# A four-stage transformer block on one core: products of a fast matrix multiplication summed in PSUM by twos, the feed-forward norms transposed by TensorE, and a new instruction order

## The chip, the core and the metric

The kernel runs on one core of a Trainium2 chip. The metric is the device time of one execution in microseconds, lower is better; the figure for the kernel before is the median of three runs. Everything is fp32.

## The reference

Eight sequences of 512 rows and 256 columns go through four residual stages. Each stage normalises its input without weights, and its result is added to the input.

```python
x = x + attn_a(layernorm(x))   # linear attention: l2norm(xWq) * mean over rows of (l2norm(xWk) * xWv)
x = x + ffn(layernorm(x))      # sigmoid(xr Wr) * (relu(xk Wk)**2 Wv)
x = x + attn_b(layernorm(x))   # 16 heads of 64: softmax over axis=2 of q k^T / 8, then Wl, with biases
x = x + ffn(layernorm(x))      # the same weights as the first ffn
```

In the ffn, `xr = mu_r * x + (1 - mu_r) * x_prev` and `xk` likewise, where `x_prev` is the sequence shifted down by one row. In `attn_b` the softmax is taken along the queries, so its sums belong to keys and can scale the values.

## The kernel before, in words

A sequence is called b, its two halves of 256 rows are h. Names in the profile follow the stages: `a` is the norm of the linear attention, `f` the first ffn, `n` the norm of the head attention, `g` the second ffn. `tr_g` is thus a transposed norm of a second ffn, `k_g`, `r_g` and `o_g` its three products, `kv` and `q` the products of the linear attention, `y` the output projection of the heads.

**Head attention.** Heads go in pairs g, eight pairs for each sequence, 64 in all. For each pair and each of four blocks c of 128 keys, `scores` makes a 128x1024 tile `sc` in two banks of PSUM, VectorE takes the negated maxima `nm`, ScalarE writes the exponentials `e` with their sums, GpSimd scales the values (`vs`), and `context` accumulates `cx`. `attend` issues two pairs at once, each `context` behind the next `scores`. PSUM has three double tiles (`PAIRS`) and two single ones (`BANKS`); all other products take one of these five slots.

**Seven products.** The projections to q, k and v of the heads use a fast scheme with seven products of half-size blocks in place of eight. `project_pairs` makes q and k of two pairs, `values_fast` half of a sequence's values; both call `seven`, which is run 31 + 14 times. Sums of weights are made once, sums of rows (`xts`) once for each sequence. Each product has its own bank, and its result is read and added by VectorE, ScalarE (`L780` copies product 5) and GpSimd (`L783`, `L785` add product 5 to two partial results). The last two additions are `L788` and `L792`.

**Norms.** `normed` takes statistics on VectorE, the power on GpSimd and the scaled copy on ScalarE (or on VectorE, if `early`). The result is needed transposed. `normed_t` does that by TensorE, four 128x128 transposes into a bank. `normed_dma` does it by DMA: GpSimd splits the fp32 words into 16-bit halves (`L405`), the SP queue issues a transposing DMA, ScalarE joins the halves (`L414`). In the kernel before, a0, a1, f0, f1, n0, n1 and g7 are transposed by TensorE, all others by DMA. The ffn then makes the shifted part on ScalarE (`L465`) and mixes on VectorE (`L479`), from the bank or, behind the DMA, from SBUF.

**Order.** Every queue is in order, and the program is written in one sequence by a planner. `Order` keeps a clock for each engine ("T" TensorE, "A" ScalarE, "V" VectorE, "G" GpSimd, "S" the SP queue). Every strand of work is a generator whose `yield` names the engine, a cost in us, when it can start, and optionally a mark it waits for. The planner always runs the strand that can start first, with ties broken by due times and by `CHOICES`, one triple for each double pair: a share of TensorE work, a slack, and a seed of tie-breaking numbers. `attend` calls `fill`, which puts in work that fits within a slack; between two `attend` calls, `until` and `fill` issue the strands: projections for the next pairs, norms, ffns, linear attention.

```python
for first in range(0, G, 2):
    g = order.period = first + 1
    attend(first)
    ...
    order.add(project_pairs(g + 1), g, NP)
    ...
    order.until(g, share)
```

The next `attend` starts with the scores of pair g + 1, so they wait for the last addition of `seven` for these pairs.

Of the kernel before, what the change touches and what calls it, by code (L numbers as in the profile page):

```python
# [32 lines left out]
PASS = {"T": 0.27, "A": 0.2, "V": 0.17, "G": 0.17, "S": 2.0}  # L33
# [5 lines left out]
    (1, 1, 35120), (4, 0, 43370), (-1, 0, 57790), (-2, 2, 0), (-2, 0, 0), (-2, 2, 98886),  # L39
    (-6, 0, 75181), (-4, 2, 57617), (1, 2, 0), (6, -1, 74538), (-2, 2, 93122), (0, 0, 0),  # L40
    (-1, 2, 13389), (0, 2, 5382), (4, 0, 20720), (-4, 2, 0), (4, -1, 42679), (0, 0, 80313),
    (-1, -1, 6501), (-1, 1, 49947), (-6, -1, 38303), (0, 1, 13925), (0, 0, 0), (-2, 2, 98850),
    (4, 1, 69230), (0, -1, 54519), (4, 0, 64684), (-2, 0, 15869), (2, 2, 90925), (-4, 2, 75109),
    (6, 2, 43324), (-6, 2, 0), (0, 0, 0), (2, 2, 66685),
# [3 lines left out]
class Steps:  # L48

# [9 lines left out]
    def advance(self, end):  # L59
        try:  # L60
            step = self.gen.send(end)
        except StopIteration:
            self.live = False
            return
        self.live = True
        self.on, self.cost, self.ready = step[:3]
        self.gate = step[3] if len(step) > 3 else -1
        self.mark = step[4] if len(step) > 4 else None

# [5 lines left out]
class Order:  # L75
# [5 lines left out]
    def __init__(self):  # L81
        self.free = {"T": 0.0, "A": 0.0, "V": 0.0, "G": 0.0, "S": 0.0}
        self.chains, self.period, self.spent, self.count = [], -1, 0.0, 0
        self.marks = {None: 0.0}

        self.banks = [0.0] * (PAIRS + BANKS)
        self.current, self.at = None, 0.0
# [40 lines left out]
    def give(self):  # L128

        self.banks = [self.ended if c is self.current else c for c in self.banks]  # L130

    def ready(self, c):
        ready = max(c.ready, self.marks[c.mark])
        if c.on == "T":
            slots = self.slots(self.now)
            if slots:
                ready = max(ready, slots[0][0])
        return ready
# [4 lines left out]
    def run(self, c):  # L143
        if c.on == "T":
            self.spent += c.cost
        outer = self.current, self.at
        self.current, self.at = c, self.now
        end = self.ended = self.place(c.on, c.cost, self.ready(c))
        c.advance(end)
        self.current, self.at = outer  # L150
        if not c.live:
            self.chains.remove(c)

    def able(self, most=99.0):

        return [
            c for c in self.chains
            if c.mark in self.marks and c.gate <= self.period
            and (c.on != "T" or c.cost <= most and self.slots(self.now))
        ]  # L160
# [61 lines left out]
    def finish(self):  # L222
        self.period = 10**6
        while self.chains:
            self.run(self.first(self.able()))
# [3 lines left out]
def kernel(ctx: ExitStack, tc: tile.TileContext, a: dict, out: bass.AP):  # L229
# [119 lines left out]
    def normed(src, name, s, h, ready, early=False):  # L349
# [8 lines left out]
        if early:  # L358

            ready = yield "G", 1.05, ready  # L360
            nc.gpsimd.tensor_scalar(rstd, mv[:, :, 1], LN_EPS, 1.0, ALU.add, ALU.mult)
            nc.gpsimd.tensor_tensor(rstd, rstd, neg_half[:, :2], ALU.pow)
            ready = yield "V", 0.75, ready
            for u in range(2):
                nc.vector.tensor_scalar(
                    xn[:, u, :], src[:, 2 * h + u, :], mv[:, u, 0:1], rstd[:, u : u + 1],
                    ALU.subtract, ALU.mult,
                )
        else:

            shift = small.tile([P, 2], F32, tag="shift", name=f"shift_{name}_{h}")
            nc.vector.tensor_scalar(shift, mv[:, :, 0], -1.0, None, ALU.mult)
            ready = yield "G", 1.3, ready
            nc.gpsimd.tensor_scalar(rstd, mv[:, :, 1], LN_EPS, 1.0, ALU.add, ALU.mult)
            nc.gpsimd.tensor_tensor(rstd, rstd, neg_half[:, :2], ALU.pow)
            nc.gpsimd.tensor_tensor(shift, shift, rstd, ALU.mult)
            ready = yield "A", 1.0, ready
            for u in range(2):
                nc.scalar.activation(  # L379
                    xn[:, u, :], src[:, 2 * h + u, :], AF.Identity,  # L380
                    bias=shift[:, u : u + 1], scale=rstd[:, u : u + 1],
                )
# [15 lines left out]
    def normed_dma(src, name, s, h, ready, dst, mark=None):  # L398
# [4 lines left out]
        ready = yield "G", 1.8, ready  # L403
# [9 lines left out]
        ready = yield "A", 0.9, ready, -1, mark  # L413
        nc.scalar.copy(  # L414
# [26 lines left out]
    edge = {}  # L441

    def ffn(xb, name, s, h, ready, add_on, by_dma):


        if by_dma:
            ps = chunks(s["xr"], h)
            ready = yield from normed_dma(
                xb, name, s, h, ready,
                lambda: s["xr"].bitcast(U16)[:, h, :].rearrange("p (k s) -> p k s", k=KC),  # L450
            )
        else:
            ps, ready = yield from normed_t(xb, name, s, h, ready)

        parts = ((1, s["xn"]), (0, s["xp"]))
        if not edge:
            nc.gpsimd.tensor_scalar(fv, fv, 0.5, None, ALU.mult)
            order.place("G", 0.8, 0.0)
# [16 lines left out]
        xr, xk = chunks(s["xr"], h), chunks(s["xk"], h)  # L475
# [9 lines left out]
        if not by_dma:  # L485
            order.give()
        done = yield "T", BANK, mixed
# [32 lines left out]
    xta, vh, fronts, begun = {}, {}, set(), set()  # L520
# [29 lines left out]
    def linear(b, h):  # L550
# [4 lines left out]
        if b < 2:  # L555
            ps, ready = yield from normed_t(xb, f"a{b}", s, h, ready, early=True)
            ready = yield "A", 0.5, ready
            nc.scalar.copy(xt, ps)
            order.give()
        else:  # L560
            ready = yield from normed_dma(
                xb, f"a{b}", s, h, ready, lambda: s["xp"].bitcast(U16)[:, h, :, 2:]
            )
# [72 lines left out]
    def front(b, h, gf, ready):  # L636
# [10 lines left out]
        ready = yield from ffn(xb, f"f{b}", s, h, ready, adder(b), b >= 2)  # L647
# [104 lines left out]
    def seven(name, sums, mul, c, begin, join):  # L752
# [3 lines left out]

        (c11, c12), (c21, c22) = c

        def product(n):
            ready = yield "T", FAST, 0.0, -1, sums  # L760
            ps = bank(f"m{n}_{name}")
            mul(ps, n)
            return ps.rearrange("p (u s) -> p u s", u=2), ready

        ps, ready = yield from product(1)
        u1 = yield from begin(ps, c11, ready)
        order.give()
        ps, ready = yield from product(6)
        u2 = yield "V", 0.62, max(ready, u1)
        nc.vector.tensor_tensor(c12, ps, c11, ALU.add)  # L770
        order.give()
        ps, ready = yield from product(2)
        yield "V", 0.62, max(ready, u1)
        nc.vector.tensor_tensor(c11, ps, c11, ALU.add)
        order.give()
        ps, ready = yield from product(7)
        u3 = yield from join(ps, c21, c12, max(ready, u2))
        ps, p5 = yield from product(5)
        p5 = yield "A", 0.5, p5
        nc.scalar.copy(c22, ps)  # L780
        order.give()
        u6 = yield "G", 1.3, max(p5, u2)
        nc.gpsimd.tensor_tensor(c12, c12, c22, ALU.add)  # L783
        u7 = yield "G", 1.3, max(p5, u3)
        nc.gpsimd.tensor_tensor(c22, c22, c21, ALU.add)  # L785
        ps, ready = yield from product(4)
        yield "V", 0.62, max(ready, u7)
        nc.vector.tensor_tensor(c21, ps, c21, ALU.add)  # L788
        order.give()
        ps, ready = yield from product(3)  # L790
        order.marks[name] = max(u7, (yield "V", 0.62, max(ready, u6)))
        nc.vector.tensor_tensor(c12, ps, c12, ALU.add)  # L792
        order.give()
# [9 lines left out]
    def project_pairs(g):  # L803

        b, p = divmod(g, NP)
        lhs = [
# [6 lines left out]
        def mul(ps, n):  # L813
            for w in range(2):
                nc.tensor.matmul(  # L815
                    ps[:, w * HS : (w + 1) * HS], lhsT=lhs[w][n - 1], rhs=block_of_rows(b, n),
                    start=True, stop=True,
# [10 lines left out]
        def join(ps, dst, part, ready):  # L828
# [6 lines left out]
            order.give()  # L835
# [5 lines left out]
    def values_fast(b, half):  # L841


        rhs = blocks_of_weights(av, blocks["sums_v"], split_values, half)
        yield "G", 0.0, 0.0, -1, ("vs", NP * (b - 1) + 3 + 4 * half, 1)
        v = vh[b, half] = one.tile([P, NT, 512], F32, tag=f"v{half}", name=f"v_{b}_{half}")

        def mul(ps, n):
            for u in range(2):
                nc.tensor.matmul(  # L850
                    ps[:, u * HS : (u + 1) * HS], lhsT=block_of_rows(b, n)[:, u * P : (u + 1) * P],
                    rhs=rhs[n - 1], start=True, stop=True,
# [12 lines left out]
        def join(ps, dst, part, ready):  # L865
            ready = yield "V", 0.62, ready
            nc.vector.tensor_tensor(dst, ps, part, ALU.add)
            order.give()
            ready = yield "G", 1.3, ready
            nc.gpsimd.tensor_tensor(dst, dst, spread(dvb[:, half, :]), ALU.add)  # L870
# [49 lines left out]
    def tail(b, h, ready):  # L920
# [4 lines left out]
        yield from ffn(x[b], f"g{b}", buffers(not last), h, ready, add_on, not last)  # L925
# [111 lines left out]
    def attend(g):  # L1037

        for c in range(NT):
# [8 lines left out]
            order.fill(0.0, 2.8)  # L1048
        for c in range(NT):
# [8 lines left out]
            order.fill(0.0, 2.8)  # L1058
# [29 lines left out]
    total -= 6 * 3.3 + 7 * 1.1  # L1088
    total += 2 * FAST
    for first in range(0, G, 2):  # L1090
# [3 lines left out]
        order.place("T", CHANGE, 0.0)  # L1094
        for h in range(2):
# [69 lines left out]
```

## Time and profile before

| What | Value |
|---|---|
| median of 3 runs | 1161.8 us (1161.39 to 1164.65) |
| profiled execution | 1162.71 us, its span 1160.8 us |
| granted TensorE clock, mean | 0.994 |
| matmul passes | 7012 |
| transposing DMAs (`DMA_TRANSPOSE`), 3.1 us to landing | 50 |

The page of the profile gives the busy time of every engine; the groups of instructions have a line of the kernel, an engine, an operation, the tiles out<-in, a count, busy us and the mean ns of one. An fp32 matmul is shown as two passes, a transpose as one. The ends of matmuls are modelled, so their starts are the firmer figure. A wait is put down to what ended it.

### The profile page before, as it was taken

To read this page: it belongs to the slowest core of one execution; us is meant where nothing else is said; L and a number is where in the kernel's file an instruction comes from. 1 tells how busy PE (TensorE), PEld (TensorE's weight loads), DVE (VectorE), ACT (ScalarE), POOL (GpSimd) and SP (SyncE) were. 2 spreads that over 40 slices of the span, in tenths; PEclk is the share of its full clock that TensorE was granted. 3 is DMA by queue.
4 is the path that set the end of the run, shared out by engine and by line. 5 is a ranking of instruction groups with operands and counts; after the bars stand their busy time and mean duration, and the time that the engine had idled before them with its cause. 6 is when DMAs were issued, how large, how long until landed. Compare 5 with 4: busy or idle time off the path is not lost.

```text
span 1160.8 us, 19186 instructions
## 1 busy us (share of the span) xinstructions
PE 1129.8 (97%) x7012; PEld 703.9 (61%) x7012; DVE 806.4 (69%) x1384; ACT 730.6 (63%) x1802; POOL 485.7 (42%) x702
## 2 busy tenths in 40 slices
PE   6999899999999999999999999999999999999997
PEld 3646466655668566656666655766657655666556
DVE  5676776777866767776886667676776777656853
ACT  3666575677855767657585568456774776556643
POOL 5465434443337334345532444442546343433211
PEclk9999899999999999999999999999999999999999
DMA  8000000110102100012000120001110100000001
GB/s 294 1 1 19 1 19 2 28 20 9 19 1 64 37 1 19 1 46 38 10 10 10 46 38 1 10 19 37 24 32 15 24 11 10 19 10 11 10 1 37
DMA packets 63294, 29.17 MB, mean 25 GB/s; under 512 B 53568, under 2 KB 61760, under 8 KB 62688
## 3 DMA queue, kind: packets, MB, share of 16 engines
q1 hardware_dynamic: 62048, 26.22, 9.4%
q8 instruction: 56, 0.92, 0.3%
q10 hardware_dynamic: 864, 1.05, 0.3%
q0 software_dynamic: 288, 0.67, 0.2%
q14 instruction: 38, 0.31, 0.1%
HBM read 10.63 MB, written 4.19 MB: 13 GB/s over the span
## 4 chain that ended last, share of the span: by engine, by line
PE 46%; DVE 2%; issue 1%; ACT 1%; DVEq 0%
PE cx L1024 10%; PE sc L971 10%; PE m_qk L815 8%; PE y L426 5%; PE m_v L850 4%; PE r_g L426 2%; PE o_g L426 2%; PE k_g L491 1%; PE r_f L426 1%; PE kv L571 1%; PE o_f L426 1%; PE k_f L491 1%; PE q L426 1%; DVE xrFalse L479 1%; DVE xrTrue L479 0%
## 5 line engine op out<-in xcount | busy, mean ns | idle before, releaser
L987 ACT ACTIVATE e<-sc,nm 128x512 f32<-128x512 f32 x512 | 346.6, 690 | 126.7 <-DVE nm L976 125.5
L976 DVE TENSOR_REDUCE nm<-sc 128x2 f32<-128x1024 f32 x256 | 307.9, 1216 | 60.9 <-PE sc L971 60.5
L971 PE MATMUL sc<-qk 64*64 64x512 f32 x2048 | 270.5, 600 | 9.4 <-DVE qk L792 8.3
L1024 PE MATMUL cx<-e,vs 64*64 64x512 f32 x2048 | 268.2, 594 | 0.2 <-POOL vs L1004 0.2
L1004 POOL TENSOR_TENSOR vs<-v,rs 128x256 f32<-128x256 f32 x128 | 78.5, 614 | 383.2 <-DVE rs L1000 363.3
L1024 PEld LDWEIGHTS cx<-e,vs 64*64 64x64 f32 x2048 | 85.4, 134 | 139.9 <-issue 115.9
L971 PEld LDWEIGHTS sc<-qk 64*64 64x64 f32 x2048 | 73.8, 133 | 151.4 <-issue 82.7
L426 PE MATMUL y<-al,ctx 128*128 128x256 f32 x512 | 116.3, 380 | 0.0
L426 PEld LDWEIGHTS y<-al,ctx 128*128 128x128 f32 x512 | 96.8, 190 | 17.3 <-ACT e L987 3.2
L987 ACT ACTIVATION_READ_ACCUMULATOR e<-sc,nm 128x1 f32 x512 | 105.6, 206 | 0.0
L1032 DVE TENSOR_TENSOR ctx<-cx,ctx 128x512 f32<-128x512 f32 x64 | 44.2, 691 | 48.0 <-ACT ctx L1031 46.9
L571 PE MATMUL kv<-wkv,xpFalse 128*128 128x512 f32 x112 | 52.4, 607 | 1.1 <-ACT xpFalse L414 1.1
L783 POOL TENSOR_TENSOR qk<-qk,qk 128x512 f32<-128x512 f32 x31 | 40.8, 1315 | 27.8 <-ACT qk L780 26.2
L913 DVE TENSOR_TENSOR x<-y,x 128x512 f32<-128x512 f32 x32 | 22.1, 689 | 39.9 <-PE y L426 39.7
L405 POOL COPY xrFalse<-xnFalse 128x512 uint16<-128x512 uint16 x72 | 42.6, 626 | 8.1 <-ACT xnFalse L379 8.1
L1031 ACT COPY ctx<-cx 128x512 f32<-128x512 f32 x64 | 37.5, 585 | 12.3 <-PE cx L1024 12.3
L517 POOL TENSOR_TENSOR x<-x,xkFalse 128x512 f32<-128x512 f32 x24 | 31.0, 1293 | 29.5 <-DVE xkFalse L510 21.9
L785 POOL TENSOR_TENSOR qk<-qk 128x512 f32<-128x512 f32 x31 | 40.6, 1310 | 2.4
L815 PE MATMUL m_qk<-xts,aq 128*128 128x256 f32 x124 | 37.1, 381 | 3.9 <-DVE v L788 3.9
L815 PE MATMUL m_qk<-xta,aq 128*128 128x256 f32 x124 | 38.2, 390 | 0.0
L770 DVE TENSOR_TENSOR qk<-m_qk,qk 128x512 f32<-128x512 f32 x31 | 21.4, 691 | 23.9 <-PE m_qk L815 23.3
L815 PE MATMUL m_qk<-xta,sums_q 128*128 128x256 f32 x124 | 36.9, 379 | 0.0
(248 smaller groups left out, 2037.5 us busy)
## 6 DMA issues: line engine op xcount, KB each, us to landing
out<-x SPq DMA_DIRECT2D x16, 256.0 KB, 2.1
x<-in_x SPq DMA_DIRECT2D x6, 512.0 KB, 4.3
aq<-in_aq SPq DMA_DIRECT2D x1, 1024.0 KB, 7.9
ak<-in_ak SPq DMA_DIRECT2D x1, 1024.0 KB, 9.9
av<-in_av SPq DMA_DIRECT2D x1, 1024.0 KB, 11.9
al<-in_al SPq DMA_DIRECT2D x1, 1024.0 KB, 14.3
xkFalse<-xrFalse SPq DMA_TRANSPOSE x36, 3.1
x<-in_x SPq DMA_DIRECT2D x4, 128.0 KB, 4.3
```

The costliest lines, as they stand in the source:

```text
L405: nc.gpsimd.tensor_copy(apart.rearrange("p (l k u d) -> p l k u d", l=2, k=KC, u=2)[:, :, :, u, :], s["xn"].bitcast(U16)[:, h, u, 2:].rear ...
L426: nc.tensor.matmul(ps[:, u * D : (u + 1) * D], lhsT=lhs[i][:, u * P : (u + 1) * P], rhs=rhs[i], start=(i == 0), stop=(i == n - 1),)
L571: nc.tensor.matmul(ps, lhsT=xt[:, kc, u * P : (u + 1) * P], rhs=wkv[:, kc, :], start=(kc == 0), stop=(kc == KC - 1),)
L783: nc.gpsimd.tensor_tensor(c12, c12, c22, ALU.add)
L815: nc.tensor.matmul(ps[:, w * HS : (w + 1) * HS], lhsT=lhs[w][n - 1], rhs=block_of_rows(b, n), start=True, stop=True,)
L850: nc.tensor.matmul(ps[:, u * HS : (u + 1) * HS], lhsT=block_of_rows(b, n)[:, u * P : (u + 1) * P], rhs=rhs[n - 1], start=True, stop=True,)
L971: nc.tensor.matmul(ps[m * HD : (m + 1) * HD, j, :], lhsT=kt[hs, keys], rhs=qt[hs, :], start=True, stop=True,)
L976: nc.vector.tensor_reduce(nm, ps, AX.X, ALU.max, negate=True)
L987: nc.scalar.activation(e[:, j, :], ps[:, j, :], AF.Exp, bias=nm[:, j : j + 1], accum_out=sums[g, h][:, c % 2, j : j + 1],)
L1004: nc.gpsimd.tensor_tensor(vs, vh[b, p // 4][:, 2 * h : 2 * h + 2, cols].rearrange("p t (j d) -> p t j d", j=2), rs.unsqueeze(3).to_broadca ...
L1024: nc.tensor.matmul(cx[m][j * HD : (j + 1) * HD, :], lhsT=vsc[g, c // 2][ks, c % 2, j, :], rhs=es[g, c][ks, j, :], start=(c == 0), stop=(c ...
L1032: nc.vector.tensor_tensor(ct, cx[1], ct, ALU.add)
```

## The change

In `seven`, product 2 is added by TensorE onto product 1 in the same bank after product 1 has been read, product 4 onto 7 and product 3 onto 5. The copy of product 5 and the two GpSimd additions are gone; three results are read twice instead, once before and once after the second product. Three banks are held for longer, and the second product of each waits for the reading of the first. For the values, the bias difference is added by GpSimd once, to a partial sum, instead of behind each join.

The norms of all ffns (f and g) and of a2 are now transposed by TensorE; a3 to a7 and n2 to n7 keep the DMA, and GpSimd instead of ScalarE joins their halves. f0 and f1 take the `early` path of `normed`. The negated mean `shift` is made by GpSimd instead of VectorE. A second ffn of a sequence waits, in the plan, for that of the sequence before. `attend` fills with a slack of 1.0 instead of 2.8, strands with a gate open only after the `attend` of their period, and the list `CHOICES` is another one, so that nearly all instructions between the attentions stand in a new order. A further function `mixed_dma` is in the file but is not called, as every ffn passes `by_dma=False`.

```diff
-PASS = {"T": 0.27, "A": 0.2, "V": 0.17, "G": 0.17, "S": 2.0}
+PASS = {"T": 0.27, "A": 0.2, "V": 0.17, "G": 0.17, "S": 2.2}
...
 CHOICES = (
-    (1, 1, 35120), (4, 0, 43370), (-1, 0, 57790), (-2, 2, 0), (-2, 0, 0), (-2, 2, 98886),
...
+    (-4, 2, 90203), (-4, -1, 82533), (0, 0, 0), (2, 2, 84393), (2, 0, 0), (-2, 2, 72979),
...
-            if c.mark in self.marks and c.gate <= self.period
-            and (c.on != "T" or c.cost <= most and self.slots(self.now))
+            if c.mark in self.marks and c.gate <= self.open
+            and (c.on != "T" or c.cost <= most) and (not c.takes or self.slots(self.now))
...
-            nc.vector.tensor_scalar(shift, mv[:, :, 0], -1.0, None, ALU.mult)
-            ready = yield "G", 1.3, ready
+            ready = yield "G", 1.4, ready
+            nc.gpsimd.tensor_scalar(shift, mv[:, :, 0], -1.0, None, ALU.mult)
...
-        ready = yield "A", 0.9, ready, -1, mark
-        nc.scalar.copy(
+        ready = yield "G", 1.25, ready, -1, mark
+        nc.gpsimd.tensor_copy(
             dst().rearrange("p k (s l) -> p l k s", l=2),
             turned.rearrange("p (l k s) -> p l k s", l=2, k=KC),
         )
...
+        ps, ready = yield from normed_t(xb, name, s, h, ready, early=name in ("f0", "f1"))
...
-        if b < 2:
-            ps, ready = yield from normed_t(xb, f"a{b}", s, h, ready, early=True)
+        if b < 3:
+            ps, ready = yield from normed_t(xb, f"a{b}", s, h, ready, early=b < 2)
...
-        ready = yield from ffn(xb, f"f{b}", s, h, ready, adder(b), b >= 2)
+        ready = yield from ffn(xb, f"f{b}", s, h, ready, adder(b), False)
...
-        ps, ready = yield from product(1)
-        u1 = yield from begin(ps, c11, ready)
-        order.give()
-        ps, ready = yield from product(6)
+        i1, b1, ps1, ready = yield from product(1)
+        u1 = yield from begin(ps1, c11, ready)
+        i6, _, ps6, ready = yield from product(6)
         u2 = yield "V", 0.62, max(ready, u1)
-        nc.vector.tensor_tensor(c12, ps, c11, ALU.add)
-        order.give()
-        ps, ready = yield from product(2)
-        yield "V", 0.62, max(ready, u1)
-        nc.vector.tensor_tensor(c11, ps, c11, ALU.add)
-        order.give()
-        ps, ready = yield from product(7)
-        u3 = yield from join(ps, c21, c12, max(ready, u2))
-        ps, p5 = yield from product(5)
-        p5 = yield "A", 0.5, p5
-        nc.scalar.copy(c22, ps)
-        order.give()
-        u6 = yield "G", 1.3, max(p5, u2)
-        nc.gpsimd.tensor_tensor(c12, c12, c22, ALU.add)
-        u7 = yield "G", 1.3, max(p5, u3)
-        nc.gpsimd.tensor_tensor(c22, c22, c21, ALU.add)
-        ps, ready = yield from product(4)
-        yield "V", 0.62, max(ready, u7)
-        nc.vector.tensor_tensor(c21, ps, c21, ALU.add)
-        order.give()
-        ps, ready = yield from product(3)
-        order.marks[name] = max(u7, (yield "V", 0.62, max(ready, u6)))
-        nc.vector.tensor_tensor(c12, ps, c12, ALU.add)
-        order.give()
+        nc.vector.tensor_tensor(c12, ps6, c11, ALU.add)
+        order.give(i6)
+        i7, b7, ps7, p7 = yield from product(7)
+        u3 = yield from join(ps7, c22, c12, max(p7, u2), True)
+        p2 = yield "T", FAST, u1, -1, None, False
+        mul(b1, 2, False)
+        yield from begin(ps1, c11, max(p2, u2))
+        order.give(i1)
+        i5, b5, ps5, p5 = yield from product(5)
+        c22_done = yield "V", 0.62, max(p5, u3)
+        nc.vector.tensor_tensor(c22, ps5, c22, ALU.add)
+        p4 = yield "T", FAST, u3, -1, None, False
+        mul(b7, 4, False)
+        yield from join(ps7, c21, c12, p4, False)
+        order.give(i7)
+        p3 = yield "T", FAST, c22_done, -1, None, False
+        mul(b5, 3, False)
+        order.marks[name] = yield "V", 0.62, p3
+        nc.vector.tensor_tensor(c12, ps5, c12, ALU.add)
+        order.give(i5)
...
-        def join(ps, dst, part, ready):
+        def join(ps, dst, part, ready, first):
+            both = v[:, 0:2, 256:]
+            if first:
+                ready = yield "G", 1.3, ready
+                nc.gpsimd.tensor_tensor(both, part, spread(dvb[:, half, :]), ALU.add)
             ready = yield "V", 0.62, ready
-            nc.vector.tensor_tensor(dst, ps, part, ALU.add)
-            order.give()
-            ready = yield "G", 1.3, ready
-            nc.gpsimd.tensor_tensor(dst, dst, spread(dvb[:, half, :]), ALU.add)
+            nc.vector.tensor_tensor(dst, ps, both, ALU.add)
...
-        yield from ffn(x[b], f"g{b}", buffers(not last), h, ready, add_on, not last)
+        if not last:
+
+            ready = yield "V", 0.0, ready, -1, ("g", b - 1, h) if b else ("n1", h)
+        order.marks["g", b, h] = yield from ffn(x[b], f"g{b}", buffers(not last), h, ready, add_on, False)
...
-            order.fill(0.0, 2.8)
+            order.fill(0.0, 1.0)
```

## The prediction

> **What bounds the kernel now.** I read the page's first part, then the waits of TensorE, then TensorE's matmul starts, and last the timelines of all engines around the two longest holes.
>
> ```profile
> PE 1129.8 (97%) x7012; PEld 703.9 (61%) x7012; DVE 806.4 (69%) x1384; ACT 730.6 (63%) x1802; POOL 485.7 (42%) x702
> ```
> TensorE is the bound: no other engine is over 69%. But 97% is busy time with modelled ends. The starts say more. An undisturbed pass (an fp32 product is two) steps on by 0.429 us for 512 columns, 0.2155 us for 256, 0.109 us for a transpose of 128; four 64x64 passes share one 0.429 us. With 4,096 quarter-array, 176 wide, 2,684 half-wide passes and 56 transposes that makes 439.6 + 75.6 + 578.5 + 6.1 = 1,099.8 us of pure stream. The span is 1,160.8: 6.3 before the first matmul, about 6.7 behind the last, and **48 us of holes**: 6.5 in the first 58 us, then 13.1 in 126 crumbs under 0.16 us, 2.6 in middling ones, and 23.5 in only 24 holes of 0.3 us or more. Those 24 are what a change of order or latency can win.
>
> The waits of TensorE name the longest:
>
> ```profile
> PE sc L971 <- DVE qk L792: 8.3, 5, 3.4
> PE m_qk L815 <- DVE v L788: 3.9, 2, 2.0
> ```
> Columns: sum, times, longest. L788 and L792 are the last two additions of the seven products; the scores, or a bank, wait for them. Around the second longest hole:
>
> ```profile
> 573.64 1.89 PE L491 MATMUL k_g<-xkTrue,fk 128*128 128x256 f32 x8
> 578.03 1.98 PE L971 MATMUL sc<-qk 64*64 64x512 f32 x8 [2.50 <-DVE qk L792]
> ...
> 572.35 1.24 DVE L372 TENSOR_SCALAR shift_f<-mv_f 128x2 f32<-128x2 f32 x1
> 573.50 1.64 DVE L479 SCALAR_TENSOR_TENSOR xrTrue<-xrTrue,mu,xpTrue 128x256 f32<-128x256 f32 x2
> ...
> 576.70 0.68 DVE L788 TENSOR_TENSOR qk<-m_qk,qk 128x512 f32<-128x512 f32 x1
> 577.30 0.68 DVE L792 TENSOR_TENSOR qk<-m_qk,qk 128x512 f32<-128x512 f32 x1
> ...
> 570.95 1.27 POOL L783 TENSOR_TENSOR qk<-qk,qk 128x512 f32<-128x512 f32 x1
> 572.30 1.26 POOL L785 TENSOR_TENSOR qk<-qk 128x512 f32<-128x512 f32 x1
> ```
> TensorE was through by 575.4. The two additions came at 576.7 because VectorE was full of slow small work: a 128x2 operation took 1.24 us where its median is 0.17. The hole costs twice, since the clock then drops:
>
> ```profile
> 134.00:140.00 6.00, 5.46 (x28) 1.76 (x32) 2.89 (x7) 1.45 (x4) 2.42 (x5) 0.50 0.01 3
> 578.00:581.00 3.00, 2.96 (x16) 1.04 (x20) 2.62 (x3) 0.00 (x0) 2.65 (x4) 0.50 0.03 5
> ```
> These are the stretches behind the 3.6 us and the 2.7 us hole: granted clock 0.50, third number from the end.
>
> [...]
>
> ```profile
> L479 DVE SCALAR_TENSOR_TENSOR xrTrue<-xrTrue,mu,xpTrue x28: 470/860/1498, 288.6 to 1084.6; 128x256 f32<-128x256 f32 x28
> L479 DVE SCALAR_TENSOR_TENSOR xrFalse<-tr_g,mu,xpFalse x4: 473/474/474, 1141.2 to 1147.2; 128x256 f32<-128x256 f32 x4
> ```
> (ns min/median/max.) The same mix takes up to 1,498 from SBUF, and 474 always with one input in PSUM. [...] the trace has accumulating passes at the same 0.2155 us, but no read in mid-sum.
>
> **The change part by part.**
>
> *Transposes to TensorE, on the path.* Fourteen norms, of two halves each, leave the DMA path (a2, f2 to f7, g0 to g6). Each half adds four transposes:
>
> ```profile
> 1138.22 0.44 PE tr_g L393 x4
> ```
> 28 x 0.436 = **+12.2 us** of stream, with nothing to hide it: 1,112.0 in all. The products keep their matmul count (14 each, in 45 sevens).
>
> *Beside it.* VectorE: the 104 SBUF mixes at L479 take 80.3 us; at 0.477 each 49.6, so −30.7. The shifts of L372 leave (−18.2). A qk seven swaps two additions for one addition and a pair of joins (−0.69 + 0.87, times 31: +5.7); a values seven gains one (14 x 0.69: +9.7). 806 becomes some 773. ScalarE: 45 copies L780 (−26.3) and 50 joins L414 of 1.34 (−67.1) go; 62 second biases of 0.42 (+26.1) and two copies of 0.6 for a2 come: 731 becomes 665. GpSimd: L783 and L785 go (−118.3), as do 56 of 100 copies L405 (−33.0); 22 joins come, not in the trace, taken as twice the 0.62 of a copy half as large (+27.3; bounds 0.6 to 1.34, ScalarE's price: 13 to 30), and 56 shifts at about 0.2 (+11): 486 becomes 373. On SP, 28 of 50 transposing DMAs go; DMA engines were 9% busy, so I take nothing for them. All this lies beside TensorE and counts only through holes. The norms that keep the DMA have time in the new order: n2 to n7 over 26 us of stream from the ffn's last product to their first use, a4 to a7 over 80 from the tail that frees their x. The path itself (add, statistics, scale, two copies, 3.1 us of DMA, join, four sums of rows) is some 14 us by its rows, so a GpSimd join is covered unless GpSimd is some 12 us behind.
>
> *What goes.* Holes at L788 and L792: 3.60 + 2.67 + 2.21 + 2.03, and 1.13 and 0.96 in front of other scores, 12.6 in sum. The GpSimd additions ahead of them, the two-input mixes and the shift are all gone. The half-clock steps behind the two longest (0.90, 0.85, 0.85, 0.47; 0.90, 0.59) are 4.6. Of the remaining 6.3 us in twelve holes I take half (3.2), for engines with 4 to 23% less to do and, by the smaller slack in attend, nothing but exps, ctx copies and scale work inside the attention. **−20.4 us**; between −8 (only half of the 12.6 + 4.6 goes) and −30 (crumbs too).
>
> *What is late next.* TensorE now waits within a seven: product 2 for the bias's read of 1, product 4 for the join's read of 7, product 3 for the addition that reads 5. Behind each stands the whole TensorE queue. In the built order the stream between is at least 3.45 us for 1 to 2, 1.72 for 7 to 4 and 0.86 for 5 to 3 (medians 6.0, 5.2, 2.6 in the qk sevens). The price of the link is in the trace:
>
> ```profile
> 1081.94 0.59 PE L815 MATMUL m_qk<-xta,sums_k 128*128 128x256 f32 x2
> 1082.37 1.89 PE L426 MATMUL r_g<-fr,xrTrue 128*128 128x256 f32 x8
> ...
> 1082.57 0.69 DVE L792 TENSOR_TENSOR qk<-m_qk,qk 128x512 f32<-128x512 f32 x1
> ```
> 0.20 after the slot's end, 0.68 to work, some 0.05 to the waiting matmul: 0.94 us, so cover of 1 us suffices where VectorE is free. At three of the 31 ends the new order has no other stream between the last product and the scores (for pairs 6, 12 and 60; before there was one, the 3.6 us hole): 0.94 each at 12 and 60; at 6 the join (0.20 + 0.88) and four statistics (1.08) stand ahead of the last addition (0.68 + 0.05), 2.89 against 0.86 of stream, so 2.0. With 0.2 for 5 to 3: **+4.1**. Bounds: 2, and 15 if each of the 135 in-seven waits lacks 0.1 us. A transposed half now holds one of the five bank slots for some 3 us (four ScalarE biases of 0.48, four mixes of 0.44), and a pair of products for 2 to 9 us instead of about 1.5. The trace of before has no such hold, so its cost is unknown: nothing, if the order's plan holds; I leave it in the upper bound.
>
> *Sum*: 12.2 + 4.1 − 20.4 = **−4.1 us**. The profiled execution (1,162.7 us, its span and 1.9 around it) would become 1,158.6; it stands 0.9 above the median of 1,161.8, whose counterpart is **1,157.7 us**.
>
> **The rivals.**
>
> *Nothing but waits exchanged (slower).* The mechanism is TensorE standing inside the sevens, at products 2, 4 and 3. For: ScalarE and VectorE serve exps and maxima of 0.69 and 1.22 us first in first out, so an answer may be a microsecond late. Against: the covers above. At 0.1 us for each of 135 it is 13.5: 1,157.7 − 0.2 + 13.5 = about 1,171; it decides from (20.4 − 12.2 − 3.9) / 135 = 0.03 us each, where the gain is gone, and gives a loss of 0.3% from 0.06.
>
> *Half the holes stay (same).* They move to other places, as VectorE at 66% still has bursts: 1,166 at −12 instead of −20.4, 1,162 where four fifths of the 20.4 go.
>
> *A clean schedule (faster by more).* Only start, crumbs and the three bare ends stay: holes 6.5 + 13.1 + 4.1, so 1,161.8 + 12.2 + 4.1 − 26.1 = 1,152; with half the crumbs gone 1,145.
>
> *The transposes not costing 12.2*: excluded, as TensorE has no cheaper place for them and no engine's bound lies above it.
>
> **How the numbers follow.** The forecast has 0.35 and the clean schedule 0.13, both mostly beyond 0.3% (3.5 us, about what a measurement of this kernel can tell from no change): faster 0.47. Half the holes staying, with the near side of the forecast: same 0.24. Waits in the sevens: slower 0.29. The range leaves out a tenth on each side: 1,148 (clean, a third of the crumbs gone) to 1,169 (0.08 us per in-seven wait).
>
> **What would show it.** Right: transposes x168 at 0.109 in the starts; no two-input mix over 0.5 us; no hole over 2.5 us and no clock of 0.50 after 58 us; GpSimd near 373, ScalarE near 665, VectorE near 773 busy; scores waiting for the last addition at pairs 6, 12, 60. Wrong: TensorE waiting at m_qk or m_v for the bias, join or addition with over 5 us in all, or for a bank that a transposed half holds; or new half-clock stretches.

## The result, and the profile after

| | before | after |
|---|---|---|
| median of seven runs each | 1161.79 us (1160.82 to 1164.65) | 1158.85 us (1158.24 to 1159.85) |
| profiled execution | 1162.71 us, span 1160.8 us | 1158.33 us, span 1156.6 us |
| granted TensorE clock, mean | 0.994 | 1.000 |

The ratio is 0.9971, with a 95% interval of 0.996 to 0.9983: 2.9 us faster, just inside the 0.3% that was set as the edge of what can be told from no change. The forecast was 1,157.7.

The first part of the page of the kernel after, in the columns of that of before:

```profile
PE 1134.6 (98%) x7124; PEld 716.1 (62%) x7124; DVE 774.7 (67%) x1377; ACT 664.7 (57%) x1763; POOL 376.7 (33%) x630
```

VectorE, ScalarE and GpSimd lost 32, 66 and 109 us of work. TensorE, the bound, got 112 transposes more. So the three engines' 207 us were worth only what they took out of TensorE's holes. By matmul starts, counted as for the kernel before (the prediction's 1,099.8 and 1,112.0 are the same streams with rounded steps):

| TensorE, us | before | after |
|---|---|---|
| pure stream | 1,099.7 | 1,111.9 |
| holes in the first 58 us | 6.5 | 7.2 |
| holes of 0.3 us and more behind that | 23.5 in 24 | 9.0 in 8 |
| everything smaller | 18.1 | 17.0 |
| tail behind the last matmul | 6.7 | 5.3 |

The stream's +12.2 stands against −14.9 of holes and −1.4 of tail. The longest hole after the start-up is now 1.56 us instead of 3.60. The waits of TensorE in the kernel after (sum, times, longest):

```profile
PE sc L1019 <- DVE qk L832: 3.1, 3, 1.4
PE m_qk L858 <- DVE qk L824: 1.3, 1, 1.3
PE cx L1072 <- DVE v L915: 1.1, 1, 1.1
...
PE m_v L894 <- ACT qk L866: 0.7, 1, 0.7
...
PE m_qk L858 <- ACT qk L866: 0.7, 1, 0.7
```

`L832` is the last addition of the seven for q and k, where before it was L792. It still holds back scores, but three times and 1.4 us at most, not five times and 3.4. The other rows are new in kind. `L824` adds product 5 (the read before product 3), `L866` is the bias's read of product 1, for which product 2 or a bank waits, and `L915` a join of the values, for which a context waits. TensorE now stands inside the sevens. The two-input mixes are gone from VectorE, as the group of mixes in the kernel after shows (ns min/median/max, first and last start in us):

```profile
L478 DVE SCALAR_TENSOR_TENSOR xrFalse<-tr_f,mu,xpFalse x28: 468/474/478, 33.6 to 947.1; 128x256 f32<-128x256 f32 x28
```

Maximum 478 ns, where the same mix took up to 1,498. And the half clock is gone up to the last matmul. Here is the stretch that held the longest hole, first in the kernel before, then in the kernel after (length; busy time of PE, PEld, DVE, ACT, POOL; granted clock, DMA share, GB/s). The granted clock rises from 0.94 to 1.00, and its mean over the whole execution is 1.000:

```profile
116.00:174.00 58.00, 54.57 (x362) 31.39 (x358) 42.15 (x64) 36.37 (x94) 23.32 (x31) 0.94 0.05 10
116.00:174.00 58.00, 55.34 (x370) 32.23 (x366) 37.39 (x63) 33.00 (x96) 17.96 (x31) 1.00 0.00 1
```

The largest new stall is at the end of the seven for pair 6. The timeline of the kernel after, first TensorE, then VectorE (start, us, engine, line, operation):

```profile
158.26 0.59 PE L858 MATMUL m_qk<-xts,ak 128*128 128x256 f32 x2
160.11 0.70 PE L858 MATMUL m_qk<-xta,sums_q 128*128 128x256 f32 x2 [1.26 <-DVE qk L824]
160.65 0.59 PE L858 MATMUL m_qk<-xta,sums_k 128*128 128x256 f32 x2
162.64 1.09 PE L1019 MATMUL sc<-qk 64*64 64x512 f32 x8 [1.39 <-DVE qk L832]
...
156.77 2.69 DVE L685 SCALAR_TENSOR_TENSOR xkFalse<-xkFalse,rnq,gf 128x256 f32<-128x256 f32 x4
159.38 0.68 DVE L824 TENSOR_TENSOR qk<-m_qk,qk 128x512 f32<-128x512 f32 x1
159.98 0.86 DVE L874 SCALAR_TENSOR_TENSOR qk<-m_qk,dbias,qk 128x256 f32<-128x256 f32 x2
160.77 0.41 DVE L361 BATCH_NORM_STATS2 st_f<-x 128x6 f32<-128x256 f32 x1
...
161.84 0.66 DVE L832 TENSOR_TENSOR qk<-m_qk,qk 128x512 f32<-128x512 f32 x1
```

TensorE stops twice. At the scores it waits behind the join and four statistics, as forecast (1.56 us by the starts, told 2.0). Before that, at product 3, it waits for `L824`, which is queued behind four operations of the linear attention that take 2.69 us; this 1.42 us was not forecast.

### The profile page after: what moved, and what is told of

It reads as the page before. It is cut to its first block, busy times and chain, and to the rows that moved or that the text cites. A ratio compares the mean times of both kernels' runs of the same rounds, so it can differ in the third digit from the quotient of the medians.

```text
span 1156.6 us, 19060 instructions
## 1 busy us (share of the span) xinstructions
PE 1134.6 (98%) x7124; PEld 716.1 (62%) x7124; DVE 774.7 (67%) x1377; ACT 664.7 (57%) x1763; POOL 376.7 (33%) x630
## 4 chain that ended last, share of the span: by engine, by line
PE 94%; DVE 3%; ACT 1%; POOL 1%; issue 1%; DMA 0%; DVEq 0%; ACTq 0%; POOLq 0%
PE sc L1019 19%; PE cx L1072 19%; PE m_qk L858 16%; PE y L432 9%; PE m_v L894 7%; PE kv L613 4%; PE o_f L432 2%; PE o_g L432 2%; PE k_g L533 2%; PE r_g L432 2%; PE r_f L432 2%; PE q L432 2%; PE k_f L533 2%; DVE xkFalse L685 1%; PE qk L991 1%; PE tr_g L399 1%
## 5 line engine op out<-in xcount | busy, mean ns | idle before, releaser
L1019 PE MATMUL sc<-qk 64*64 64x512 f32 x2048 | 264.6, 593 | 3.1 <-DVE qk L832 3.1
L1072 PE MATMUL cx<-e,vs 64*64 64x512 f32 x2048 | 262.4, 590 | 1.1 <-DVE v L915 1.1
L866 ACT ACTIVATE qk<-m_qk,bias 128x256 f32<-128x256 f32 x124 | 52.4, 479 | 60.2 <-PE m_qk L858 60.0
L874 DVE SCALAR_TENSOR_TENSOR qk<-m_qk,dbias,qk 128x256 f32<-128x256 f32 x124 | 54.2, 478 | 24.9 <-PE m_qk L858 24.0
L619 ACT COPY av<-kv 128x256 f32<-128x256 f32 x32 | 11.9, 373 | 46.0 <-PE kv L613 43.7
L858 PE MATMUL m_qk<-xta,sums_k 128*128 128x256 f32 x124 | 36.9, 379 | 0.0
## 6 DMA issues: line engine op xcount, KB each, us to landing
al<-in_al SPq DMA_DIRECT2D x1, 1024.0 KB, 14.9
```

The lines of the kernel that those rows point to most:

```text
L858: nc.tensor.matmul(ps[:, w * HS : (w + 1) * HS], lhsT=lhs[w][n - 1], rhs=block_of_rows(b, n), start=start and w == 0, stop=True, skip_grou ...
L866: nc.scalar.activation(dst[:, w, :], ps[:, w, :], AF.Identity, bias=bias[:, w, p : p + 1])
L874: nc.vector.scalar_tensor_tensor(dst[:, w, :], ps[:, w, :], dbias[:, w, p // 2 : p // 2 + 1], part[:, w, :], ALU.add, ALU.add,)
L1019: nc.tensor.matmul(ps[m * HD : (m + 1) * HD, j, :], lhsT=kt[hs, keys], rhs=qt[hs, :], start=True, stop=True,)
L1072: nc.tensor.matmul(cx[m][j * HD : (j + 1) * HD, :], lhsT=vsc[g, c // 2][ks, c % 2, j, :], rhs=es[g, c][ks, j, :], start=(c == 0), stop=(c ...
```

## The experiments

The three parts of the change (the sum in PSUM, the norms on TensorE, the order) were taken apart. Where a plan had to be made anew, the text says whether with the same list of choices or with a list drawn for that kernel. In the kernels planned anew, except the one with the shifted part in PSUM and the last one, the planner's `clear` also looks over its banks again after each step; for the kernel after this gives the same program.

**The transposes' price, twice.** The kernel after in its own order, with every one of the 28 halves that came to TensorE transposed a second time.

```diff
-        for kc in range(KC):
+        again = name == "a2" or name[0] == "f" and int(name[1]) >= 2 or name[0] == "g" and int(name[1]) < 7
+        for _ in range(2 if again else 1):
+            for kc in range(KC):
...
```

> The changed kernel with the same instruction order, but the four transposes of each of the 28 newly added halves (a2, f2 to f7, g0 to g6) are issued twice, onto the same columns. TensorE's stream grows by 28 x 0.436 = 12.2 us. Theory (the stream is the bound and nothing hides the transposes): +12.2 us less at most 1 us taken from holes, so 1158.9 + 11 to 12 = 1170 to 1171. Rival (the transposes sit in holes that exist anyway): +0 to +5, so under 1164.

1172.66 us, ratio to before 1.0087 (1.0074 to 1.0101): 13.8 us over the kernel after, some 2 us more than the 11 to 12 that were expected. The stream grew by 12.2 and the holes by 2.0. Nothing hid the second transposes.

**Additions left out of the kernel before.** All else, the order too, stands; two terms are missing from the products.

```diff
-        nc.gpsimd.tensor_tensor(c12, c12, c22, ALU.add)
...
-        nc.gpsimd.tensor_tensor(c22, c22, c21, ALU.add)
```

> The kernel before, same instruction order, without the two GpSimd additions of each seven (L783 and L785): two of the four blocks of every fast product lack product 5, so its output is not the reference's. GpSimd loses 118 us, and the last two additions wait only for their own products. Theory (GpSimd's additions[...] made most of the large holes): mixes shrink towards 0.48 us, the four holes of 2 to 3.6 us and their half-clock stretches mostly go, 1161.3 minus 7 to 12 = 1149 to 1154. Rival (VectorE's own load and the order made them): at most 3 us, 1158 to 1161.

1144.14 us, ratio 0.9851 (0.9838 to 0.9865): 17.1 us faster than the kernel before, whose median beside these runs was 1161.21, and more than theory and rival said. The first part of its page, and its mixes:

```profile
PE 1122.5 (98%) x7012; PEld 704.0 (62%) x7012; DVE 772.3 (68%) x1384; ACT 730.5 (64%) x1802; POOL 370.6 (32%) x612
```

```profile
L479 DVE SCALAR_TENSOR_TENSOR xrTrue<-xrTrue,mu,xpTrue x28: 471/478/948, 283.1 to 1066.1; 128x256 f32<-128x256 f32 x28
```

VectorE has the same 1,384 instructions and is busy 34 us less (806.4 before). In the group shown, still with two SBUF inputs, the median fell from 860 to 478 ns. Its three sister groups had medians of 482 to 546 before, and long mixes among them. All 104 mixes from SBUF together were busy 52.9 us instead of 80.3, which is 27.4 of the 34 us. In the trace of the kernel before, the long ones all ran beside an instruction of GpSimd: the 34 of the 104 that had none beside them took 470 to 486 ns, the other 70 a median of 917 and up to 1,541 ns. The 13 mixes with an input in PSUM that had one beside them took 484 ns at most. What holds the slow ones up isn't shown; the run shows what the additions cost in this kernel. The holes of TensorE fell from 48.1 to 29.5 with the transposes still on the DMA path: this one edit takes out more than the whole change did (33.2).

Was it the chain through GpSimd, or the VectorE that its additions slowed? The trace of the kernel before answers this for the longest holes. Ahead of the one at 1,080.5 us:

```profile
1075.45 1.33 POOL L785 TENSOR_TENSOR v<-v 128x512 f32<-128x512 f32 x1
...
1075.16 1.90 DVE L479 SCALAR_TENSOR_TENSOR xkTrue<-xrTrue,mu,xnTrue 128x256 f32<-128x256 f32 x2
1076.98 2.90 DVE L479 SCALAR_TENSOR_TENSOR xrTrue<-xrTrue,mu,xpTrue 128x256 f32<-128x256 f32 x2
1079.81 0.68 DVE L788 TENSOR_TENSOR v<-m_v,v 128x512 f32<-128x512 f32 x1
```

GpSimd's last addition to this tile was done at 1,076.8, but `L788` came 3.0 us later, behind four mixes that took 4.8 us. It is the same at all six holes that the prediction put down to `L788` and `L792`: `L785` was done 0.2 to 3.1 us before `L788` began, and VectorE was busy right up to it. What ended last there was VectorE's queue. Elsewhere VectorE did wait for `L785`, 15.3 us in seven waits.

**The shift moved alone.** The kernel before in its order, with the negated mean made by GpSimd.

```diff
-            nc.vector.tensor_scalar(shift, mv[:, :, 0], -1.0, None, ALU.mult)
...
+            nc.gpsimd.tensor_scalar(shift, mv[:, :, 0], -1.0, None, ALU.mult)
```

> The kernel before, same order, with the 128x2 shift made by GpSimd instead of VectorE (L372), as in the change. VectorE loses 18 us of which 7 were waiting. Theory: a part of the hole of 2.7 us at 575 us goes, 1 to 3 us in all, 1158 to 1160. Rival (no hole depends on it): within 0.5 us of before; or slower, where the power on GpSimd starts later by 0.2 us, by under 1 us.

1158.36 us, ratio 0.9987 (0.9975 to 0.9999). By the ratio 1.5 us are gained, within the expectation, though VectorE is busy 17 us less (789.1). The four longest holes hardly shrank in its profile, from 3.60, 2.67, 2.21 and 2.03 to 3.46, 2.41, 1.99 and 2.02. The 13 executions spread from 1157.4 to 1163.3 us, and the granted clock goes with them: 0.996 or 0.997 in the seven up to 1158.4, 0.993 in two at about 1160, 0.992 in the four at about 1163.2. The profiled one is of the last. It has two half-clock stretches that the profile of the kernel before lacks, at 30 us and here, first in the kernel before, then in this one:

```profile
1081.00:1084.00 3.00, 3.00 (x16) 2.52 (x14) 2.18 (x7) 0.42 (x1) 0.00 (x0) 1.00 0.00 0
1081.00:1084.00 3.00, 3.00 (x8) 2.33 (x8) 0.94 (x2) 0.59 (x2) 0.00 (x0) 0.50 0.00 0
```

The hole ahead of it is 2.03 us long before and 2.02 here, so much the same hole was followed by half a clock in one execution and not in the other. Why isn't shown.

**GpSimd's load put back without the chain.** The kernel after with two additions of the same size per seven on a scratch tile, for which nobody waits.

```diff
+        for _ in range(2):
+            nc.gpsimd.tensor_tensor(scratch, scratch, scratch, ALU.add)
```

> The changed kernel, same order, with two more GpSimd additions of 128x512 on a scratch tile in each of the 45 sevens, at the place where before had its two; nothing waits for them. GpSimd's work returns to about 490 us. Theory (it is the chain through GpSimd and the two-input mixes that cost; the mixes now have one SBUF input and the chain is gone): within 1.5 us of the changed kernel, 1158 to 1160.5. Rival (GpSimd's load alone delayed scaled values, powers and joins): 3 to 8 us slower, 1162 to 1167.

1161.35 us, ratio 0.9995 (0.9987 to 1.0004): 2.5 over the kernel after, between the two expectations. GpSimd is busy 468.8 us, 92 more, and VectorE 777.7, only 3 more: the mixes read one input from PSUM now (57 of the 128 in the kernel after ran beside GpSimd, and none took over 486 ns). So here, where nobody waits for it and the mixes do not read two inputs from SBUF, the load alone cost 2.5 us.

**The order alone.** The kernel after with the list of choices of the kernel before.

```diff
-    (-4, 2, 90203), (-4, -1, 82533), (0, 0, 0), (2, 2, 84393), (2, 0, 0), (-2, 2, 72979),
+    (1, 1, 35120), (4, 0, 43370), (-1, 0, 57790), (-2, 2, 0), (-2, 0, 0), (-2, 2, 98886),
...
```

> The changed kernel with the list of choices of before, nothing else changed: same stream of 1112.0 us, same work on all engines, another order. Theory (the order is a part of the gain that cannot be separated from the rest: 3 large holes or 20 depend on it): slower, 1170 to 1245, with TensorE waiting for banks at the first context of a pair and for last additions. Rival (the steps themselves hold the gain, any order of this planner keeps it): 1156 to 1163.

1251.79 us, ratio 1.078 (1.0764 to 1.0797). This is over the upper end of what was expected. The stream is the same to the pass; the holes are 126 us. Its longest waits of TensorE:

```profile
PE sc L1018 <- ACT e L1034: 13.7, 4, 12.1
PE cx L1071 <- POOL vs L1051: 13.2, 3, 8.1
...
PE m_qk L857 <- POOL aq L755: 8.0, 1, 8.0
```

One list, drawn for another set of strands, costs 93 us. Every comparison of plans has to reckon with that.

**Three parts undone with the same list.** These ran before the order's weight was known. First the seven of the kernel before, with the rest of the kernel after:

```diff
-        i1, b1, ps1, ready = yield from product(1)
-        u1 = yield from begin(ps1, c11, ready)
+        ps, ready = yield from product(1)
+        u1 = yield from begin(ps, c11, ready)
+        order.give()
...
```

> The changed kernel with the seven products of before: own bank for each, ScalarE copies product 5, GpSimd adds it twice; the norms stay as changed. The order is planned anew, with the same choices. Stream unchanged at 1112.0 us. Theory (the holes came from the GpSimd additions and the two-input mixes together): about half of the 17 us of holes at the last additions comes back, 1163 to 1168. Rival 1 (mixes and transposes' side alone made the holes): no more than 2 us above the changed kernel, 1158 to 1161. Rival 2 (the order is what counts, any new order loses): over 1170.

1237.74 us, ratio 1.0653 (1.0638 to 1.0667), as the second rival had it. Then the kernel after with f2 to f7 and g0 to g6 by DMA, joined by GpSimd, and mixed either from SBUF or, by the function that the change left uncalled, with the shifted part in PSUM:

```diff
-        ready = yield from ffn(xb, f"f{b}", s, h, ready, adder(b), False)
+        ready = yield from ffn(xb, f"f{b}", s, h, ready, adder(b), b >= 2)
...
-        order.marks["g", b, h] = yield from ffn(x[b], f"g{b}", buffers(not last), h, ready, add_on, False)
+        order.marks["g", b, h] = yield from ffn(x[b], f"g{b}", buffers(not last), h, ready, add_on, not last)
```

> The changed kernel with the norms of f2 to f7 and g0 to g6 transposed by DMA again and mixed from SBUF, two SBUF inputs; GpSimd joins the halves, the products stay summed by twos. The order is planned anew. Stream 1100.6 us, 11.3 less. Theory ([...] late mixes open holes): mixes of 0.5 to 1.5 us return, 8 to 14 us of holes come back, so 1156 to 1162, no gain worth having. Rival (transposes are simply 11 us of bound, the products did all the good): 1147 to 1150.

> As the run with mixes from SBUF, but ScalarE writes the shifted part to a PSUM bank, so that the mix has one SBUF input only (the function that lies unused in the changed kernel). Stream 1100.6 us. Theory: mixes stay at 0.48 us and do not lengthen under GpSimd's work, so at least 3 us faster than the run with mixes from SBUF, 1150 to 1157, if the ten or so more bank holds cost nothing. Rival ([...] bank holds stall TensorE): equal to that run or slower, 1158 to 1166.

1204.45 us (ratio 1.0373, 1.0355 to 1.039) and 1198.06 us (1.0315, 1.0301 to 1.0329). These two are far from their expectations. The longest waits touch the edits (19.1 us of scores behind the last addition of the old seven in the first run, 17.7 us of contexts behind the mixes in the last), but the list alone can cost 93 us, more than any of the three lost. So their times say nothing of the parts.

Their mixes do say something. GpSimd joined the halves in both, and the mixes of the two, their order apart, differ only in where the shifted part lies. Here are a group with both inputs from SBUF and the same group with one in PSUM:

```profile
L484 DVE SCALAR_TENSOR_TENSOR xrTrue<-xrTrue,mu,xpTrue x28: 452/479/1506, 245.1 to 1166.1; 128x256 f32<-128x256 f32 x28
L514 DVE SCALAR_TENSOR_TENSOR xrTrue<-xrTrue,mu,prev_g x28: 473/478/482, 284.0 to 1160.7; 128x256 f32<-128x256 f32 x28
```

With one input in PSUM none of the 104 mixes took over 482 ns. That is the direct test of what the second SBUF input costs.

**The same parts, each with a list drawn for it.** The old seven with the norms on TensorE:

> The run with the seven products of before and the changed norms, but with a list of choices drawn anew for it, by the same means as for the run with the norms by DMA. Stream 1112.0 us. Theory (in its own order the GpSimd additions still cost holes, as a longer chain, but few[...]): 1162 to 1172, so 70 us of the first run with the old products were order alone. Rival (the products' chain costs dozens of us whatever the order): over 1200.

1164.44 us, ratio 1.0021 (1.0015 to 1.0027), as expected. Some 73 of the 79 us above the kernel after were order. Its longest waits of TensorE are a context behind an operation of an ffn (`L551`, which reads the product `o_f`) and, of the old kind, scores behind the last addition of the old seven:

```profile
PE cx L1073 <- DVE xkFalse L551: 4.2, 1, 4.2
PE sc L1020 <- DVE qk L833: 3.9, 2, 3.3
```

The new seven with f2 to f7 and g0 to g6 by DMA, joined by ScalarE as in the kernel before, and mixed from SBUF:

```diff
-        ready = yield "G", 1.25, ready, -1, mark
-        nc.gpsimd.tensor_copy(
+        ready = yield *(("A", 1.3) if by_act else ("G", 1.25)), ready, -1, mark
+        (nc.scalar.copy if by_act else nc.gpsimd.tensor_copy)(
...
```

> The changed kernel with the products summed by twos, but f2 to f7 and g0 to g6 transposed by DMA as before, joined by ScalarE as before and mixed from SBUF; the list of choices is drawn anew for it. Stream 1100.6 us. Theory (the products' sum in PSUM took the GpSimd additions away, [...] the transposes on TensorE are a price without a counterpart): the holes of the changed kernel, 33 us, and 11.3 us less stream, so 1144 to 1151, faster than both. Rival (the mixes from SBUF need TensorE's transposes, else the large holes return): 1157 or more.

**1145.78 us**, ratio 0.9855 (0.984 to 0.987), as expected: 16.0 us under before and 13.1 under after, the fastest version that computes everything. Its page's first part, a group of its mixes and its longest waits behind the start-up:

```profile
PE 1125.6 (98%) x7020; PEld 710.2 (62%) x7020; DVE 788.1 (69%) x1377; ACT 698.0 (61%) x1789; POOL 410.7 (36%) x682
```

```profile
L485 DVE SCALAR_TENSOR_TENSOR xrTrue<-xrTrue,mu,xpTrue x28: 450/477/837, 250.3 to 1108.7; 128x256 f32<-128x256 f32 x28
```

```profile
PE sc L1026 <- DVE qk L839: 2.3, 2, 1.4
PE m_qk L865 <- DVE qk L831: 1.5, 2, 1.3
```

Its stream is 1,100.6, 11.3 less than after's, and its holes are 32.5 against 33.2. The mixes read SBUF twice and still take 476 to 480 ns in the median of each group. Single ones take up to 1,437 ns, but all 104 together are busy 55.9 us, against 80.3 before and 49.6 undisturbed. So with GpSimd's additions gone they are 6.3 us above undisturbed instead of 30.7, and the norms' way through TensorE buys nothing against this version.

The same with GpSimd joining these norms:

```diff
-                by_act=True,
```

> As the run with the norms by DMA and its own choices, but GpSimd joins the ffns' halves too (26 x 1.34 us more on GpSimd, less on ScalarE), with a list drawn anew for it. Theory (GpSimd is where lateness comes from: [...] a longer queue): 3 to 9 us slower than with ScalarE's join, 1149 to 1158. Rival (ScalarE, full in the attention, is the worse place): as fast or faster, under 1148.

1158.86 us, ratio 0.9971 (0.9958 to 0.9983): 13.1 slower than with ScalarE, more than the 3 to 9 that were expected. Scores and contexts now wait for late values:

```profile
PE cx L1078 <- POOL vs L1058: 6.0, 3, 3.6
PE sc L1025 <- DVE qk L838: 3.1, 3, 1.4
PE sc L1025 <- ACT e L1041: 2.7, 1, 2.7
```

The stream is the same and the holes are 44.8 against 32.5. The first row is what a GpSimd queue with 26 more joins of 1.34 us would do, but the two orders differ, so part of the 13.1 can be order.

**How good is a list?** The kernel after with a list drawn anew:

> The changed kernel with nothing but its list of choices drawn anew, starting from its own. Stream 1112.0 us. Theory (33 us of holes are near what this planner reaches with that stream; what is left are start, crumbs and three bare ends): 0 to 4 us faster, 1155 to 1159. Rival (the order has much more to give): under 1152.

1161.06 us, ratio 0.9992 (0.9986 to 0.9999): 2.2 slower than the list of the change, where a gain was expected. So a difference of some 2 us between two lists drawn for their kernels is no finding. That is a lower bound: only seven of the 34 triples differ here, and lists that share less may differ by more.

Each with its own list, in us:

| | norms by DMA, ScalarE joins | ffn norms on TensorE |
|---|---|---|
| old seven | 1161.8 (before) | 1164.4 |
| sum in PSUM | **1145.8** | 1158.9 (after) |

Down the columns the sum in PSUM wins 16.0 and 5.6. Along the rows the transposes on TensorE cost 2.7 (near what two lists can differ by) and 13.1. With the old seven the move pays back most of its 12.2, probably as the mixes then read one input from PSUM: before, they were busy 30.7 us more than undisturbed. With the new seven only 6.3 us of that are left to pay back.

Two things in the table are not clean. The kernel before alone lacks the small parts of the change (the shift and some joins on GpSimd, a2 on TensorE, the early f0 and f1, the rules of the planner), so the 16.0 and the 2.7 hold these too. And the 13.1 holds for ScalarE's joins. With GpSimd's joins the norms by DMA came to 1158.9 us, no faster than the kernel after. So, as far as two orders can be compared, what beat the transposes was the DMA together with ScalarE's join.

## Why the prediction was right

**The sum.** In the profiled execution −4.1 was forecast and −4.4 measured. The medians show −2.9, as the profile of before lies 0.9 above its median and that of after 0.5 below: the forecast carried over the first offset and took none for the second. The first has a visible side: the profile of before has a granted clock of 0.994, while 36 of 44 later executions of that kernel have 0.996 or 0.997. The gain stays just inside the edge of 0.3%; the prediction had given 0.47 to a gain beyond it and 0.24 to a change inside it.

**The stream.** +12.2 was told and counted, and doubling the transposes cost 13.8. So they have no cover.

**What goes.** −20.4 was told. All holes outside the start fell from 41.6 to 26.0, by 15.6; with the 8.1 of new stalls below, 23.7 went. (The parts that the prediction names for its 48 us add up to 45.7; the other 2.4 are in the 18.1 of the table.) The halved clock went as told, and no hole is over 1.6 us. The working took half of the smaller large holes; in the event nearly all of them went.

**What is late next: the mis-sized term.** +4.1 was told. The three bare ends came at the named pairs, 6, 12 and 60, with 1.56 + 1.04 + 0.95 = 3.55 against 3.9. Beside them stand 1.42 at product 3 of pair 6, 1.36 at a context that waits for the values' join `L915`, and 0.89 and 0.88 where the bias's read `L866` came late: 8.1 in all. The step measured the cover of each in-seven wait by stream alone and let "cover of 1 us suffices where VectorE is free" stand in for the queue of the engine that reads. The queues were not free. Ahead of `L915`, as ahead of `L824`, VectorE had four operations `L685` in a row. Ahead of `L866` at 664 us, ScalarE had the four scaled copies `L465` of a transposed half:

```profile
636.26 2.67 DVE L685 SCALAR_TENSOR_TENSOR xkFalse<-xkFalse,rnq,gf 128x256 f32<-128x256 f32 x4
638.86 0.68 DVE L915 TENSOR_TENSOR v<-m_v,v 128x512 f32<-128x512 f32 x1
...
663.01 0.85 ACT L465 ACTIVATE xnFalse<-tr_f,omu 128x256 f32<-128x256 f32 x2
663.74 0.85 ACT L465 ACTIVATE xpFalse<-tr_f,omu 128x256 f32<-128x256 f32 x2
664.45 0.87 ACT L866 ACTIVATE qk<-m_qk,bias 128x256 f32<-128x256 f32 x2
```

The underestimate of the stalls (4.0) and that of what goes (3.3, or 4.0 with the start's +0.7 and the tail's −1.4) cancel. So the mechanism was right, but that the sum came within 0.3 us of the profile is luck. The rival of waits in the sevens thus named a real mechanism, but in a few places and not 135: the unforeseen 4.6 us are as much as its decision point of 0.03 x 135 = 4, and only the larger removal kept the gain. The sign of being wrong, over 5 us of waits at `m_qk` and `m_v`, did not come: they are 2.7 us in the table of waits.

**Beside it.** Busy times hit within 4 us: 774.7, 664.7 and 376.7 against 773, 665 and 373. GpSimd's joins cost 29.3, not 27.3, at 1.34 us each. The trace of the kernel after has the read in mid-sum that the prediction did not find in that of before, and the passes on a bank that has been read step on by the same 0.2155 us: three products of each seven go onto such a bank, and of the 982 steps between neighbouring passes of the sevens 923 are 215 or 216 ns.

**What the prediction did not see** is how the parts divide. It put mixes, shift and additions into one removal. The run without the additions shows that they alone, chain and slowed mixes together, held more than the net gain, so the transposes paid 12.2 us for a relief that another part of the change brought already; the run with the norms by DMA and ScalarE's joins bears this out. At the six longest holes it was the slowed VectorE that ended last, not the chain. How the rest of the 17.1 us splits isn't settled: the shift's run shows that 17 us of VectorE's time can be worth little, but it isn't the same VectorE time.

## What to carry to other kernels

When a change has several parts that relieve the same wait, price each as if the others were in already; the second relief may find nothing and still cost its full price on the engine that is the bound. Where equal operations differ much between minimum and maximum, as the mixes here did (469 and 1,541 ns), look for another engine; taking its work away can be cheaper than moving their operand (here 1145.8 us against 1158.9). In a statically ordered program compare parts only in orders made for each, and learn first how far two such orders differ.

## What was not expected of the hardware

Two GpSimd additions per seven made VectorE busy 34 us longer without one more instruction (806.4 against 772.3), although each takes only 1.3 us and there are 90 of them: 0.38 us of VectorE time for each addition. Two additions per seven on a scratch tile in the kernel after, where the mixes read PSUM, cost VectorE 3 us in all. In these two runs the cost of GpSimd's operations thus lay in what VectorE read at that time, more than in GpSimd's own load.

Two SBUF inputs are not the whole of it: the 128x2 shift `L372`, with one, took up to 1.24 us in the kernel before, and all shifts together fell from 18.2 to 13.4 us without the additions. And a hole of TensorE of 2.0 us was once followed by half a clock, and once not.
